# A fused two-layer graph network on one core: the stores move from GpSimd's queue to SyncE's and ScalarE's

## The chip, the cores and the metric

The kernel runs on one core of a Trainium2 chip. A core has a matrix engine (TensorE, PE in the profile), three engines for elementwise work (VectorE, DVE; ScalarE, ACT; GpSimd, POOL) and SyncE (SP), which only issues transfers. Transfers between device memory and on-chip memory run on 16 DMA engines that all issuing engines share. In this program three engines issue them: SyncE, ScalarE and GpSimd. The metric is the device time of one execution in microseconds (us), lower is better. All data are float32.

## The reference, cut to what matters

The inputs are x (3327 x 512), a dense symmetric matrix adj (3327 x 3327), and the weights of two layers.

```python
h = relu(layernorm(x))
q, k, v = h @ Wq.T + bq, h @ Wk.T + bk, h @ Wv.T + bv
a = q @ k.T / sqrt(512) + adj + adj
x = x + softmax(a, axis=-1) @ v

h = relu(layernorm(x))
A2 = adj + eye
dscale = diagonal(A2) ** -0.5
temp = A2 @ h @ W.T
x = x + relu((dscale[:, None] * A2 * dscale[None, :]) @ temp)
```

Three large products have a 3327 x 3327 left operand: the softmax's numerators with h, A2 with the second h, and A2 with temp. Before the first, the scores are a product of 3327 x 512 with 512 x 3327.

## The kernel before, in words

The rows are padded to 3328, which is 26 tiles of 128 rows. Products are made in the way of Strassen and Winograd: a product of 2 x 2 blocks is done as seven block products with sums and differences of blocks before and after. VectorE makes these sums. Everything that is too large for on-chip memory goes through scratch tensors in device memory: `rowd[g]` (the right operands' rows for product g), `qd` (queries), `pd` (exponentials of the scores and their block sums), `sumd` (block sums of adj), `totd` (row totals), `t2d` (one difference of right operands, used by a later block product), `x1d` (x after the first layer). A store writes such a tensor, a load brings a part of it back later.

The stages follow each other:

* The head (L286 to L379). It makes M from the query and key weights, normalises x tile by tile (`h_transposed`; the row tile goes to `rowd[0]`, L324), transposes it, and computes the queries (`project_q`, stored at L362).
* The scores (L384 to L568). 52 steps, each a `Pair`: load two blocks of adj (`adjacency`, L418), seven products (L454), add the adjacency, exponentiate, make block sums, and store: `sum` (L446), the exponentials in four stores (L462, L481, L485, L490). At the end of each of four groups, row totals are stored (L514). The next group's queries are loaded at L399. A buffer that is loaded into for a later pair is one that an earlier pair has stored from.
* Three products (L577 to L1045), g = 0, 1, 2. Each has seven block products in the order p5, p1, p6, p7, p2, p3, p4, each of these two strips of output columns, and each strip seven steps, 294 steps in all. `run(k)` writes one step: it issues the loads of the left operand for step k+3 (`Step.load`, by `left`, L694 to L701), the matmuls of step k (L774 and L782), the sums for step k+2 on VectorE (`four_sums`, L173 to L175), and at the end of a strip the gathering of the results into the output's blocks (`Gather`, L811 to L840). Behind that come the items that `between[k]` holds: the right operand of a later strip is loaded five steps ahead and made three steps ahead (`Right`, rows loaded at L721; for p6 a store of `t2`, L746); 52 jobs that add a block of adj to a stored sum and store the result (`Job`, loads L860 and L861, add L865, store L868; they run from the second strip of g = 0 into g = 1); `attend` (residual and layernorm after g = 0, stores `x1d`, L888), `attended` (L894), `temp` (product with W, L874, store L903) and `finish` (transposes L927, relu L929, residual L930, store `out`, L931 through `store` at L92).
* After the last step, six half tiles of the output are finished, stored in turn by GpSimd and SyncE (L1044 and L1045). Row 25 holds 127 rows, and `store` writes it in two pieces, 112 and 15 rows.

The order of each engine's instructions in the scores and in the products is the order in which this program writes them: `in_order` ties each instruction to the one before it on the same engine. So an engine that has to wait with one instruction holds up all that is written behind it on that engine. Rings of buffers set when a load may start: the left operand has five buffers, its sums three; a load waits until the buffer's last reader is done.

All stores but three of the last output tiles are issued by GpSimd. SyncE issues nearly all loads. ScalarE issues 65 loads (weights and x in the head, x and `x1d` in the products). GpSimd also makes some memsets, masks and 53 small powers for the layernorms.

`general_kernel` (L1049 on) lies in a branch for other data, which isn't taken.

Of the kernel before, what the change touches and what calls it, by code (L numbers as in the profile page):

```python
# [47 lines left out]
def graph_layers_kernel(  # L48
# [38 lines left out]
        m = n - n % 16  # L87
        return [(0, m), (m, n)] if m and m < n else [(0, n)]

    def store(dst, src, n, queue=nc.gpsimd):  # L90
        for a, z in pieces(n):
            queue.dma_start(dst[a:z], src[a:z])  # L92

# [222 lines left out]
    def h_transposed(k):  # L316

        a, n = PACKS[k]
        for _, i in (o for o in order if o[0] == k):
            xt = first.pop(i) if i in first else load_x(i)  # L320
            rstd, bias = norm(xt)
            ht = n_ring([P, D], "ht")
            nc.scalar.activation(ht, xt, AF.Relu, bias=bias(), scale=rstd)
            nc.gpsimd.dma_start(rowd[0][ROW[i]], ht)  # L324
            pt = tp_bank("tp").rearrange("p (c e) -> p c e", c=DC)
            for c in range(DC):
                nc.tensor.transpose(pt[:, c], ht[:, c * P : (c + 1) * P], ident)
            w = slice((i % HALF - a) * P, (i % HALF - a + 1) * P)
            if i < HALF:
                nc.scalar.copy(hp[k][:, 0:2, :, w], pt.rearrange("p (a c) e -> p a c e", a=2))  # L330
            else:
                nc.scalar.copy(hp[k][:, 2, :, w], pt[:, 2:4])
                nc.vector.tensor_add(hp[k][:, 3, :, w], hp[k][:, 2, :, w], pt[:, 0:2])
                nc.vector.tensor_add(hp[k][:, 5, :, w], hp[k][:, 0, :, w], pt[:, 0:2])
        nc.vector.tensor_add(hp[k][:, 4], hp[k][:, 3], hp[k][:, 0])
        nc.vector.tensor_add(hp[k][:, 6], hp[k][:, 1], hp[k][:, 4])

    def project_q(k):
        a, n = PACKS[k]
        w = n * P  # L340

        qs = [half(8 + j, [P, 2, BW], "qs") for j in range(4)]

        def chain(o):
            def product(ps, name, start):
                for c in range(2):
                    nc.tensor.matmul(ps[:, :w], M[B[name]][:, c, o * P : (o + 1) * P], hp[k][:, A[name], c],  # L347
                                     start=start and c == 0, stop=c == 1, skip_group_check=True)

            def first(j, ps, sign):  # L350
                d = 2 * (j % 2) + o
                nc.scalar.activation(qs[j][:, o, :w], ps[:, :w], AF.Identity, bias=u[:, d : d + 1], scale=float(sign))

            def more(j, ps):
                nc.vector.tensor_add(qs[j][:, o, :w], qs[j][:, o, :w], ps[:, :w])

            def last():
                if o == 1:
                    for j in range(4):
                        y, z = divmod(j, 2)  # L360
                        i = ROW[y * HALF + a] * P
                        nc.gpsimd.dma_start(qd[:, 2 * z : 2 * z + 2, i : i + w], qs[j][:, :, :w])  # L362

            Chain(product, first, more, last)

        for o in range(2):
            chain(o)
# [53 lines left out]
    class Pair:  # L421
# [11 lines left out]
        def sum_of_adjacency(self, m):  # L433
# [9 lines left out]
                if d:  # L443
                    nc.vector.tensor_add(o[:, d[0]], o[:, d[0]], d[1])
            if m == 1:
                nc.gpsimd.dma_start(self.to(sumd)[:, 0:2], self.o)  # L446

        def multiply(self, qt):
            wd, g = self.wd, self.g
# [7 lines left out]
            def first(n, ps, sign):  # L457
                nc.vector.scalar_tensor_tensor(a[n], a[n], 2.0, ps[:, :wd], op0=ALU.mult,  # L458
                                               op1=ALU.add if sign > 0 else ALU.subtract)
                if n == 2:  # L460
                    nc.scalar.activation(g[1], g[1], AF.Exp, **({"bias": pad} if self.t == HALF - 1 else {}))  # L461
                    nc.gpsimd.dma_start(self.to(pd)[:, 0:2], g[1])  # L462
                beside[{0: 0, 3: 1, 1: 3, 2: 4}[n]]()

            def more(n, ps):
# [12 lines left out]
        def s1(self):  # L478
            s1 = self.g[0][:, 1]
            nc.vector.tensor_add(s1, s1, self.g[1][:, 1])  # L480
            nc.gpsimd.dma_start(self.to(pd)[:, 2:4], self.g[0])  # L481

        def s2(self):
            nc.vector.tensor_add(self.e[:, 1], self.g[0][:, 0], self.g[0][:, 1])
            nc.gpsimd.dma_start(self.to(pd)[:, 4:6], self.e)  # L485

        def s4(self):
            self.last = fours[:, self.t % 2, : self.wd]
            nc.vector.tensor_add(self.last, self.e[:, 1], self.g[1][:, 0])
            nc.gpsimd.dma_start(self.to(pd)[:, 6], self.last)  # L490

        def gather(self, m):

# [8 lines left out]
        def total(self, m, own=None):  # L502
# [8 lines left out]
            else:  # L511
                nc.vector.tensor_sub(row, ps[:1, : self.wd], acc[:1, 0])
            c0 = (STRIPS[self.s] + (1 - m) * HT[self.s]) * P + self.c
            nc.gpsimd.dma_start(totd[:, c0 : c0 + self.wd], row)  # L514


    pairs = {}
# [52 lines left out]
    def totals():  # L570
        for m in range(2):
            pairs[len(steps_of_scores) - 1].total(m, bank(ROLE["p8"], "tot"))
        nc.sync.dma_start(tot, totd[0].rearrange("(i p) -> p i", p=P))

    steps_of_scores = steps
# [87 lines left out]
    b_ring = ring(*((half, k) for k in (0, 1, 2, 3, 8, 9, 10)))  # L663
    r_ring = ring(*((half, k) for k in (4, 5, 6, 7)))
    cts = {}

    def set_up():

# [38 lines left out]
    class Right:  # L707
# [31 lines left out]
        def make(self):  # L739
# [3 lines left out]
            if r == "p6":  # L743
                nc.vector.tensor_add(own, own, self.two[:, :, 0:E])
                nc.vector.tensor_sub(own, own, self.two[:, :, E:D])
                nc.gpsimd.dma_start(self.t2[:, 0 : 2 * self.n], self.b[:, 0 : 2 * self.n])  # L746
            if r in ("p7", "p4"):
                nc.vector.tensor_sub(own, own, self.one)
            if self.n == 2:
# [100 lines left out]
    class Job:  # L850
# [13 lines left out]
        def make(self):  # L864
            nc.vector.tensor_add(self.a, self.a, self.b)  # L865
            if self.d:
                nc.vector.tensor_add(self.a[:, self.d[0]], self.a[:, self.d[0]], self.d[1])
            nc.gpsimd.dma_start(sumd[self.s][self.j][:, 2 + self.k], self.a)  # L868

    def times_weights(i, w):  # L870
        s, y, k = where(i)
# [11 lines left out]
    def attend(i):  # L883
# [1 line left out]
        xt, ps = xts[i], times_weights(i, wv_w1[0])  # L885
        nc.vector.scalar_tensor_tensor(xt, ps, rs[:, i : i + 1], xt, op0=ALU.mult, op1=ALU.add)  # L886
        nc.vector.tensor_add(xt, xt, bvs[0])
        nc.gpsimd.dma_start(x1d[i], xt)  # L888
        normed[i] = norm(xt)

    def attended(i):
        h1 = h_ring([P, D], "h1")
        nc.scalar.activation(h1, xts[i], AF.Relu, bias=normed[i][1](), scale=normed[i][0])
        nc.gpsimd.dma_start(rowd[1][i], h1)  # L894

    normed = {}

    def temp(i):
# [1 line left out]
        ps = times_weights(i, wv_w1[1])  # L900
        ts = ts_ring([P, D], "ts")
        nc.scalar.mul(ts, ps, sd[:, i : i + 1])
        nc.gpsimd.dma_start(rowd[2][i], ts)  # L903

    xrs = {}

# [9 lines left out]
            xrs[i + k] = xr[:, k]  # L916
            nc.scalar.dma_start(xr[:, k], x1d[i + k][:, 0:E])

    def finish(i, z=(0, 1), spot=None, queue=nc.gpsimd):

        s, y, k = where(i)
        n = min(P, N - i * P)
# [5 lines left out]
        o = (out_ring if spot is None else out_last)([P, D], "r")  # L928
        nc.scalar.activation(o[:, c0:c1], pt[:, c0:c1], AF.Relu, scale=sd[:, i : i + 1])  # L929
        nc.vector.tensor_add(o[:, c0:c1], o[:, c0:c1], xr[:, c0:c1])  # L930
        store(out[i * P : i * P + n, c0:c1], o[:n, c0:c1], n, queue)  # L931

    every = (*range(PAIRS), None)
    rights = {(g, r, t): Right(g, r, t) for g in range(3) for r in ORDER for t in every}
# [62 lines left out]
        rows(2, number_of(2, 4, 0, t), i, (1,))  # L997
    for n, i in enumerate(range(20, NT, 2)):
        at(number_of(2, 6, 1, 2) + n, last_load, i)
    for k, what in ((1, totals), (2, prepare), (6, prepared), (8, judge), (9, judged)):  # L1000
        at(k, what)
    at(number_of(1, 1, 0, 4), other_weights)

# [8 lines left out]
    def run(k):  # L1012
        step = steps[k]
        if k + 3 < len(steps):
            steps[k + 3].load()
        if step.t == 0:
            banks_of.update(seven())
        if not cts:
# [22 lines left out]
    with in_order(*(e.engine for e in (nc.vector, nc.tensor, nc.gpsimd, nc.scalar, nc.sync))):  # L1041
        for k in range(len(steps)):
            run(k)
        for n, i in enumerate(range(20, NT)):  # L1044
            finish(i, (0,), (0, 2, 4, 6, 7, 1)[n], (nc.gpsimd, nc.sync)[n % 2])  # L1045
    return flags[0]

@with_exitstack
def general_kernel(  # L1049
# [49 lines left out]

    def store(dst, src, n):  # L1100
        for a, z in pieces(n):
            nc.gpsimd.dma_start(dst[a:z], src[a:z])

    const = ctx.enter_context(tc.tile_pool(name="const", bufs=1))
    held = ctx.enter_context(tc.tile_pool(name="held", bufs=1))
# [316 lines left out]
```

## Time and profile before

| | |
|---|---|
| Time, median of 5 runs | 2210.8 us (2210.39 to 2214.28) |
| The profiled execution: its time | 2210.64 us |
| Its span, first to last instruction | 2208.7 us |
| TensorE clock granted | 0.996 of full speed |
| Transfers issued by SyncE, GpSimd, ScalarE | 1185, 491, 65 |
| Bytes moved | 583.68 MB, mean 264 GB/s |
| Scores, 150 to 580 us: TensorE busy, DMA share, rate | 429.43 us of 430, 0.85, 301 GB/s |
| Product g = 0, 680 to 1000 us | 318.07 us of 320, 0.88, 313 GB/s |
| 1240 to 1500 us, in product g = 1 | 258.07 us of 260, 0.88, 310 GB/s |
| 1500 to 1900 us | 400.00 us of 400, 0.60, 194 GB/s |
| Behind TensorE's last matmul, 2195 to 2208.7 us | VectorE 1.67 us, ScalarE 1.21 us busy |

The profile is of one execution. Its page gives each engine's busy time and share, the DMA queues (q1 is SyncE's, q10 ScalarE's, q0 GpSimd's, called software_dynamic), and the chain of work that ended last, followed back from the last instruction. The view of waits lists, for an engine, how long it waited for which instruction of which other engine; "SPq L697 <- PE p L782" is SyncE, standing at line 697, waiting for a matmul of line 782. A group's line gives the first and last start. The letter q behind an engine's name (SPq, POOLq) marks its sequencer, which handles waits and transfers. Issuing a transfer takes the issuing engine some time of its own; its landing comes later.

### The profile page before, as it was taken

What the parts mean: (1) busy time and instruction counts of PE and PEld (TensorE: products, weight loads), DVE (VectorE), ACT (ScalarE), POOL (GpSimd) and SP (SyncE); (2) the same over time, 40 slices, a digit from 0 to 9 for tenths busy, and PEclk for the clock granted to TensorE, in tenths of its full rate; (3) what the DMA queues carried; (4) which work ended last, traced back from release to release, by engine and by line L of the source; (5) the groups of instructions that cost most, each with busy time, mean ns of one, the idle gap of its engine ahead of it and who ended that gap; (6) DMA issues with size and microseconds to landing.
All of it is one profiled execution on the core that took longest, in us unless ns stands there. A gap on an engine that the chain in (4) does not pass through costs nothing.

```text
span 2208.7 us, 20973 instructions
## 1 busy us (share of the span) xinstructions
PE 2174.9 (98%) x6268; PEld 1166.9 (53%) x6268; DVE 1628.0 (74%) x3103; ACT 231.3 (10%) x335; POOL 357.5 (16%) x551
## 2 busy tenths in 40 slices
PE   9999999999999999999999999999999999999997
PEld 6555555455555555555454555555545555555554
DVE  6369888888877788877777778886645358777776
ACT  5321121112110000000001000000000000000011
POOL 5233333333331000001222100000000000000011
PEclk9999999999999999999999999999999999999999
DMA  8568888888969898888787899876645458766684
GB/s 286 188 209 300 298 296 281 304 284 309 353 211 327 302 370 305 280 291 315 254 307 264 307 347 354 282 275 199 219 141 181 135 189 295 248 192 191 207 305 169
DMA packets 246682, 583.68 MB, mean 264 GB/s; under 512 B 34768, under 2 KB 106270, under 8 KB 246558
## 3 DMA queue, kind: packets, MB, share of 16 engines
q1 hardware_dynamic: 192270, 399.28, 54.4%
q0 software_dynamic: 44928, 167.49, 19.9%
q10 hardware_dynamic: 9360, 15.47, 2.1%
q8 instruction: 52, 0.85, 0.2%
q14 instruction: 72, 0.59, 0.1%
HBM read 414.28 MB, written 167.85 MB: 264 GB/s over the span
## 4 chain that ended last, share of the span: by engine, by line
PE 89%; DVE 4%; DMA 3%; issue 3%; POOL 1%; ACT 0%; SPq 0%; ACTq 0%; POOLq 0%; DVEq 0%
PE p L782 53%; PE Y L454 12%; PE p L874 7%; PE Z L454 6%; PE p L774 5%; PE X L454 3%; DMA g<-in_adjT_dram 1%; PE Y L347 1%; PE mm L306 1%; DMA b<-row 1%; DVE part L173 1%; PE pt L927 0%; PE Z L347 0%; DVE part L174 0%; DMA qd<-qs 0%
## 5 line engine op out<-in xcount | busy, mean ns | idle before, releaser
L782 PE MATMUL p<-part,b 128*128 128x448 f32 (+1 forms) x3528 | 1252.3, 513 | 6.0 <-DVE part L174 4.9
L782 PEld LDWEIGHTS p<-part,b 128*128 128x128 f32 x3528 | 667.7, 190 | 569.8 <-issue 306.9
L173 DVE TENSOR_TENSOR part<-part 128x896 f32<-128x896 f32 (+1 forms) x252 | 257.2, 1021 | 99.0 <-PE p L782 46.6
L454 PE MATMUL Y<-qt,hp 128*128 128x448 f32 (+1 forms) x832 | 309.0, 514 | 3.8 <-DVE g L458 2.8
L454 PEld LDWEIGHTS Y<-qt,hp 128*128 128x128 f32 x832 | 157.2, 190 | 139.5 <-issue 72.3
L454 PE MATMUL Z<-qt,hp 128*128 128x384 f32 (+1 forms) x416 | 162.5, 513 | 0.0
L175 DVE TENSOR_TENSOR part<-part,part 128x448 f32<-128x448 f32 (+1 forms) x219 | 129.5, 591 | 16.9 <-DVE part L174 0.5
L174 DVE TENSOR_TENSOR part<-part,part 128x448 f32<-128x448 f32 (+1 forms) x219 | 129.4, 591 | 7.4
L774 PE MATMUL p<-part,b 128*128 128x448 f32 (+1 forms) x336 | 124.2, 513 | 0.0
L874 PE MATMUL p<-w,ct 128*128 128x512 f32 x272 | 123.5, 593 | 0.5 <-DVE part L886 0.5
L454 PEld LDWEIGHTS Z<-qt,hp 128*128 128x128 f32 x416 | 78.8, 190 | 67.4 <-issue 37.4
L458 DVE SCALAR_TENSOR_TENSOR g<-g,Y 128x384 f32<-128x384 f32 (+1 forms) x156 | 91.4, 586 | 28.9 <-PE Y L454 25.7
L868 POOL DMA_DIRECT2D sum<-job x52 | 28.4, 547 | 500.8 <-DVE job L865 283.4
L811 DVE TENSOR_TENSOR part<-p,part 128x384 f32<-128x384 f32 (+1 forms) x33 | 19.4, 587 | 103.9 <-PE p L782 103.1
L774 PEld LDWEIGHTS p<-part,b 128*128 128x128 f32 x336 | 63.6, 190 | 53.8 <-issue 32.4
L810 ACT COPY part<-p 128x384 f32<-128x384 f32 (+1 forms) x33 | 16.6, 503 | 682.9 <-PE p L782 682.0
L874 PEld LDWEIGHTS p<-w,ct 128*128 128x128 f32 x272 | 51.5, 190 | 59.7 <-issue 51.9
L454 PE MATMUL X<-qt,hp 128*128 128x384 f32 (+1 forms) x208 | 81.1, 512 | 0.0
L461 ACT ACTIVATE g<-g 128x768 f32<-128x768 f32 (+1 forms) x48 | 43.0, 896 | 353.5 <-DVE g L458 294.5
L446 POOL DMA_DIRECT2D sum<-o x52 | 36.9, 709 | 221.5 <-DVE o L440 152.9
L874 PE MATMUL p<-w,part 128*128 128x512 f32 x144 | 65.7, 592 | 0.0
L92 POOL DMA_DIRECT2D out_dram<-r x30 | 16.2, 542 | 302.2 <-DVE r L930 267.3
(165 smaller groups left out, 1881.7 us busy)
## 6 DMA issues: line engine op xcount, KB each, us to landing
part<-sum SPq DMA_DIRECT2D x104, 448.0 KB, 5.0
part<-p SPq DMA_DIRECT2D x91, 448.0 KB, 6.4
part<-sum SPq DMA_DIRECT2D x104, 384.0 KB, 3.5
part<-p SPq DMA_DIRECT2D x91, 384.0 KB, 4.3
part<-in_adjT_dram SPq DMA_DIRECT2D x78, 448.0 KB, 4.6
b<-row SPq DMA_DIRECT2D x234, 128.0 KB, 5.0
part<-in_adjT_dram SPq DMA_DIRECT2D x78, 384.0 KB, 3.7
g<-in_adjT_dram SPq DMA_DIRECT2D x52, 448.0 KB, 4.6
```

Source lines behind the costliest of these rows:

```text
L173: nc.vector.tensor_add(o[:, 0:2], g[:, 0:4:3], g[:, 1:2].to_broadcast([P, 2, g.shape[-1]]))
L174: nc.vector.tensor_add(o[:, 2], o[:, 1], g[:, 0])
L175: nc.vector.tensor_add(o[:, 3], o[:, 2], g[:, 2])
L306: nc.tensor.matmul(ps[r], w_q[c // 2][:, c % 2, r * P : (r + 1) * P], w_k[c // 2][:, c % 2], start=c == 0, stop=c == DC - 1)
L446: nc.gpsimd.dma_start(self.to(sumd)[:, 0:2], self.o)
L454: nc.tensor.matmul(ps[:, :wd], h_of(self.t, name, k), qt[B[name]][:, k], start=start and k == 0, stop=k == 1, skip_group_check=True)
L458: nc.vector.scalar_tensor_tensor(a[n], a[n], 2.0, ps[:, :wd], op0=ALU.mult, op1=ALU.add if sign > 0 else ALU.subtract)
L461: nc.scalar.activation(g[1], g[1], AF.Exp, **({"bias": pad} if self.t == HALF - 1 else {}))
L774: yield nc.tensor.matmul(ps[("p2", "p3", "p4", "p8")[k]][:, :w], b[:, z], a[:, 0, y], start=k == 3, stop=True)
L782: yield nc.tensor.matmul(ps[r][:, :w], b[:, i], m, start=self.t == 0, stop=self.t == PAIRS - 1 and r in ("p1", "p5", "p6", "p7"))
L868: nc.gpsimd.dma_start(sumd[self.s][self.j][:, 2 + self.k], self.a)
L874: nc.tensor.matmul(ps, cts[s][y][d][:, k * P : (k + 1) * P], w[d], start=d == 0, stop=d == DC - 1)
```

## The change

GpSimd issues no transfer any more.

* In the head and in the scores, each store is issued by SyncE at the same place in the program.
* In the products, the stores of `t2`, of the jobs, of `x1d` and of `out` are put on a list (`posted`). In the next `run`, SyncE issues them (`deliver`), behind the loads that this step issues first. The stores of h1 and ts are issued by ScalarE, which makes these rows, in place.
* The load of the row totals comes one step later than the computation that stores them.
* The six last half tiles are posted and delivered together at the end: the fourth and the fifth by ScalarE, the others by SyncE.

After it SyncE issues about 1620 transfers, ScalarE 119 and GpSimd none.

```diff
 
-    def store(dst, src, n, queue=nc.gpsimd):
+    def store(dst, src, n, queue=nc.sync):
         for a, z in pieces(n):
...
             nc.scalar.activation(ht, xt, AF.Relu, bias=bias(), scale=rstd)
-            nc.gpsimd.dma_start(rowd[0][ROW[i]], ht)
+            nc.sync.dma_start(rowd[0][ROW[i]], ht)
             pt = tp_bank("tp").rearrange("p (c e) -> p c e", c=DC)
...
                         i = ROW[y * HALF + a] * P
-                        nc.gpsimd.dma_start(qd[:, 2 * z : 2 * z + 2, i : i + w], qs[j][:, :, :w])
+                        nc.sync.dma_start(qd[:, 2 * z : 2 * z + 2, i : i + w], qs[j][:, :, :w])
 
...
             if m == 1:
-                nc.gpsimd.dma_start(self.to(sumd)[:, 0:2], self.o)
+                nc.sync.dma_start(self.to(sumd)[:, 0:2], self.o)
 
...
                     nc.scalar.activation(g[1], g[1], AF.Exp, **({"bias": pad} if self.t == HALF - 1 else {}))
-                    nc.gpsimd.dma_start(self.to(pd)[:, 0:2], g[1])
+                    nc.sync.dma_start(self.to(pd)[:, 0:2], g[1])
                 beside[{0: 0, 3: 1, 1: 3, 2: 4}[n]]()
...
             nc.vector.tensor_add(s1, s1, self.g[1][:, 1])
-            nc.gpsimd.dma_start(self.to(pd)[:, 2:4], self.g[0])
+            nc.sync.dma_start(self.to(pd)[:, 2:4], self.g[0])
 
         def s2(self):
             nc.vector.tensor_add(self.e[:, 1], self.g[0][:, 0], self.g[0][:, 1])
-            nc.gpsimd.dma_start(self.to(pd)[:, 4:6], self.e)
+            nc.sync.dma_start(self.to(pd)[:, 4:6], self.e)
 
         def s4(self):
             self.last = fours[:, self.t % 2, : self.wd]
             nc.vector.tensor_add(self.last, self.e[:, 1], self.g[1][:, 0])
-            nc.gpsimd.dma_start(self.to(pd)[:, 6], self.last)
+            nc.sync.dma_start(self.to(pd)[:, 6], self.last)
 
...
             c0 = (STRIPS[self.s] + (1 - m) * HT[self.s]) * P + self.c
-            nc.gpsimd.dma_start(totd[:, c0 : c0 + self.wd], row)
+            nc.sync.dma_start(totd[:, c0 : c0 + self.wd], row)
 
...
             pairs[len(steps_of_scores) - 1].total(m, bank(ROLE["p8"], "tot"))
+
+    def load_totals():
         nc.sync.dma_start(tot, totd[0].rearrange("(i p) -> p i", p=P))
...
     cts = {}
+    posted = []
+
+    def post(dst, src):
+        posted.append(lambda: nc.sync.dma_start(dst, src))
+
+    def deliver():
+        while posted:
+            posted.pop(0)()
 
...
                 nc.vector.tensor_sub(own, own, self.two[:, :, E:D])
-                nc.gpsimd.dma_start(self.t2[:, 0 : 2 * self.n], self.b[:, 0 : 2 * self.n])
+                post(self.t2[:, 0 : 2 * self.n], self.b[:, 0 : 2 * self.n])
             if r in ("p7", "p4"):
...
                 nc.vector.tensor_add(self.a[:, self.d[0]], self.a[:, self.d[0]], self.d[1])
-            nc.gpsimd.dma_start(sumd[self.s][self.j][:, 2 + self.k], self.a)
+            post(sumd[self.s][self.j][:, 2 + self.k], self.a)
 
...
         nc.vector.tensor_add(xt, xt, bvs[0])
-        nc.gpsimd.dma_start(x1d[i], xt)
+        post(x1d[i], xt)
         normed[i] = norm(xt)
 
     def attended(i):
         h1 = h_ring([P, D], "h1")
         nc.scalar.activation(h1, xts[i], AF.Relu, bias=normed[i][1](), scale=normed[i][0])
-        nc.gpsimd.dma_start(rowd[1][i], h1)
+        nc.scalar.dma_start(rowd[1][i], h1)
 
...
         nc.scalar.mul(ts, ps, sd[:, i : i + 1])
-        nc.gpsimd.dma_start(rowd[2][i], ts)
+        nc.scalar.dma_start(rowd[2][i], ts)
 
...
 
-    def finish(i, z=(0, 1), spot=None, queue=nc.gpsimd):
+    def finish(i, z=(0, 1), spot=None, queue=nc.sync):
 
...
         nc.vector.tensor_add(o[:, c0:c1], o[:, c0:c1], xr[:, c0:c1])
-        store(out[i * P : i * P + n, c0:c1], o[:n, c0:c1], n, queue)
+        posted.append(lambda: store(out[i * P : i * P + n, c0:c1], o[:n, c0:c1], n, queue))
 
...
         at(number_of(2, 6, 1, 2) + n, last_load, i)
-    for k, what in ((1, totals), (2, prepare), (6, prepared), (8, judge), (9, judged)):
+    for k, what in ((1, totals), (2, load_totals), (2, prepare), (6, prepared), (8, judge), (9, judged)):
         at(k, what)
...
             steps[k + 3].load()
+        deliver()
         if step.t == 0:
...
             run(k)
+        deliver()
         for n, i in enumerate(range(20, NT)):
-            finish(i, (0,), (0, 2, 4, 6, 7, 1)[n], (nc.gpsimd, nc.sync)[n % 2])
+            finish(i, (0,), (0, 2, 4, 6, 7, 1)[n], nc.scalar if n in (3, 4) else nc.sync)
+        deliver()
     return flags[0]
```

The one other store, in `general_kernel`, moves from GpSimd to SyncE in the same way.

More of the change, by code (lines that the diff above doesn't have):

```diff
@@ L1101, in store @@
         for a, z in pieces(n):
-            nc.gpsimd.dma_start(dst[a:z], src[a:z])
+            nc.sync.dma_start(dst[a:z], src[a:z])
     const = ctx.enter_context(tc.tile_pool(name="const", bufs=1))
```

## The prediction

> **What bounds the kernel now.** I read the page first: which engine is full, who carries the transfers, and the chain that ended last.
>
> ```profile
> PE 2174.9 (98%) x6268; PEld 1166.9 (53%) x6268; DVE 1628.0 (74%) x3103; ACT 231.3 (10%) x335; POOL 357.5 (16%) x551
> q1 hardware_dynamic: 192270, 399.28, 54.4%
> q0 software_dynamic: 44928, 167.49, 19.9%
> PE 89%; DVE 4%; DMA 3%; issue 3%; POOL 1%; ACT 0%; SPq 0%; ACTq 0%; POOLq 0%; DVEq 0%
> ```
>
> TensorE is busy for 98% of the span, so a change that touches no matmul can act in two ways only: through the few microseconds in which TensorE waits, and through what lies before its first and behind its last matmul. POOL has 1% of the chain, and q0, GpSimd's queue, carries all the stores. The second view is what TensorE's idle time waited for:
>
> ```profile
> PE p L782 <- DVE part L174: 4.9, 4, 1.9
> PE pt L927 <- DVE part L840: 3.1, 2, 2.5
> PE Y L454 <- DVE g L458: 2.8, 4, 1.1
> PE Y L347 <- ACT qs L352: 1.8, 1, 1.8
> ```
>
> The first number is the total in us, then the times and the longest one. All releasers are VectorE or ScalarE; no wait here is charged to a store. The third view is the end, by the groups of the program's closing lines and the timeline:
>
> ```profile
> 2194.42 2.25 DVE L930 TENSOR_TENSOR r<-r,xr 128x256 f32<-128x256 f32 x6 [1.04 <-ACT r L929]
> 2195.24 2.33 SPq L92 DMA_DIRECT2D out_dram<-r  x4
> 2196.60 0.55 POOL L92 DMA_DIRECT2D out_dram<-r  x1 [0.19 <-issue]
> ...
> L1418 SPq EVENT_SEMAPHORE  x8: 17/17/17, 2200.2 to 2201.4; - x8
> L1418 POOLq INC_SWDGE_SEM  x1: 1516/1516/1516, 2200.9 to 2200.9; - x1
> ...
> L1414 SPq EVENT_SEMAPHORE  x14: 17/28/28, 2202.4 to 2208.7; - x14
> L1414 POOLq DRAIN  x3: 40/107/5459, 2202.5 to 2208.5; - x3
> ```
>
> The last result is ready at 2196.67 and SP's last store (15 rows) is issued at 2197.09. SP has seen its stores land by 2201.4, starts its final waits at 2202.4 when GpSimd has closed its software transfers (a 1.516 us instruction), and is done at 2203.17. Then everything waits for one GpSimd DRAIN of 5.459 us, 2202.45 to 2207.91, and 0.83 us of barrier end the span at 2208.74. So 13.7 us lie behind the last matmul (2194.96), and 5.5 of them are this DRAIN.
>
> The fourth view is what SP, the engine that gets the stores, waits for today:
>
> ```profile
> SPq L418 <- DMA p<-g: 441.0, 48, 48.3
> SPq L697 <- PE p L782: 316.2, 131, 9.2
> SPq L860 <- DMA sum<-job: 31.5, 9, 7.8
> SPq L573 <- DMA totd<-acc: 25.7, 1, 25.7
> ```
>
> SP spends most of its time waiting for a buffer to come free; it has time to issue more, but it issues in order.
>
> **The change part by part.** The sum is made against the profiled execution: 2210.64 us, span 2208.7 and 1.94 around it. It stands 0.16 below the median of 2210.8.
>
> *The end.* Removed: GpSimd's three last stores, the 1.516 us closing instruction, the software completions SP waits for (4 of its 12 final ones). Added: one more store on SP, two on ScalarE. SP's list becomes rows 0, 1, 2 and the two pieces of the last tile; its stores cost 0.34 to 0.47 us and the results come every 0.37 us, so the 15-row piece is again issued near 2197.1 and seen by 2201.4. Then eight waits, which now stand 0.06 us apart (2202.37, 2202.43, ...): 2201.4 + 0.07 + 8 x 0.06 + 0.06 = 2202.0, and 0.83 of barrier: 2202.85, which is 5.9 less. This needs the DRAIN to be short. If it keeps its 5.46 us but starts when GpSimd has nothing left (2197.1), it ends at 2202.5 and the end is 2203.4: 5.3 less. If it keeps them and comes behind SP's last wait, 2202.0 + 5.46 + 0.83 = 2208.3: 0.4 less. The other DRAIN rows of GpSimd, behind no transfers, take 40 and 107 ns; they are nearest, and I take -5.8, bounds -5.9 and -0.4.
>
> *The head.* 26 row stores (0.58 us each on GpSimd) and 16 query stores (0.72 us) go to SP, whose nearest issue, the query load, costs 0.42. The TensorE wait of 1.8 us at 96 us is a chain: four query stores, the query load (SP issues it at 91.7), ScalarE's use of it at 96.4, which holds up L352. Four issues at 0.42 for 0.72 bring the load forward by up to 1.2 us. Against it: the loads of x now stand in SP's queue behind the row stores, and in the new order some are 2 to 8 us later between 28 and 40 us, where VectorE would lag by up to 4 us; TensorE waited 0.5 to 0.7 there twice. Bounds -1.2 and +3; I take -0.4, as the row of the wait is a measured one and the lag has a lead before it.
>
> *The scores.* Five stores a step, 260 in all, and 8 of totals: 5 x 0.4 = 2.0 us of SP in a step of 10 us, in which SP waits 441/52 = 8.5 us for L418. They come in the order in which the results come, so no load waits for a store that is not yet computed; a store may wait behind a load for a landing of 3 to 4 us (GpSimd's score stores land in 3.4 us by the median), and the buffers it frees are wanted a step, 10 us, later. Cover: that step. Bounds: -4.4 (all the idle time TensorE has between 579 and 651 us) and +3 (as many waits of 0.6 to 1.1 again); I take 0. The totals' load goes one step later; it held SP for 25.7 us (L573), but its stores, now on SP too, hold it as long: 0.
>
> *The products.* 52 job stores, 21 of t2 and, from attend and finish, 26 and 27 more are issued by SP after the next step's loads. A store that isn't computed yet now blocks the loads behind it. I put the new order of SP's queue against the old times at which each store was issued: at some 30 places loads come 3 to 13 us later, the worst near 788 us, where loads of the right operand go from 788.4 to 795.6 behind a t2 and a job store. They are needed at 798.3, at a time when transfers are slow:
>
> ```profile
> 770.00:800.00 30.00, 30.00 (x81) 15.20 (x80) 26.63 (x51) 0.53 (x1) 3.78 (x7) 1.00 1.04 406
> 800.00:850.00 50.00, 50.00 (x147) 27.74 (x146) 43.77 (x77) 0.48 (x1) 2.16 (x4) 1.00 0.98 354
> 1300.00:1340.00 40.00, 40.00 (x114) 21.37 (x113) 35.96 (x69) 0.48 (x1) 5.26 (x10) 1.00 1.04 403
> ```
>
> (Columns: window, length, busy time of PE, its weight loads, DVE, ACT and POOL, clock, DMA share, GB/s.) The DMA engines are full here, and VectorE has 11% of its time left at 770 to 800. What late loads cost TensorE is not in the trace. From above: at five places (805, 881, 912, 1423, 1455 us, changes of strip) VectorE finishes only 0.1 to 3 us before TensorE needs it; 3 us lost at each is +15. From below 0, and the nearest row says so: SP is blocked in just this manner already, by L860, which waits 7.79 us at 972.4 and 4.54 at 1255.7 for a job store to land; TensorE has no idle time in the 50 us after either. At 1449.8 it waits 7.01, and TensorE loses 0.86 at 1455. I take +1 for blocking. Stores also get dearer: q0 moves 167.49 MB in 19.9% (8.4 MB a point), q1 399.28 in 54.4% (7.3), so 15% more for 19.9 points, 3 of 100; over the 150 us or so that are full that is 4.5 us of transfer, of which TensorE's lead takes most: +0.5, bounds 0 and 4.5, within the +15. The 26 stores of h1 and 26 of ts on ScalarE, which is 10% busy, delay nothing on a path: 0.
>
> The Trainium skill, "DMA: Bandwidth & Descriptors", section "Queues, rings and completion order", speaks against the change: an engine takes turns between queue rows packet by packet, while within one row descriptors are taken in ring order, so loads that today run beside a store would stand behind it. The share of 1.04 at 770 us with both queues active doesn't contradict it, and no run here shows one row alone. By that rule a 448 KB store at 400 GB/s is an estimated 1.1 us ahead of the loads; at the five thin places that is 5 us more, and the sum would be about 2211.
>
> Sum: 2210.64 - 5.8 - 0.4 + 0 + 1.5 = 2205.9, with the 0.16 to the median 2206.1; I say 2206.0.
>
> **The rivals.**
> *Blocked loads decide (slower side).* In the p6 and p7 strips of the first two products SP stands in front of an uncomputed store, the right operands and sums come late to a VectorE that has 11 to 20% to spare, and TensorE waits at the changes of strip. For: the thin leads and the full windows. Against: the L860 row. Seven to ten waits of 1.5 to 2 us are 10 to 20: 2206.0 - 1.5 + (10 to 20), or 2214 to 2224. It decides from 6.2 us on, where it eats the whole gain of the end and the head.
> *The DRAIN stays.* It is GpSimd's own closing work, paid whatever it did, and comes last: 2210.64 - 0.4 - 0.4 + 1.5 = 2211.3. For: nothing in the trace ties it to transfers. Against: the 40 and 107 ns rows.
> *All goes well.* End -5.9, head -1.2, and the score waits shrink by half of 4.4, nothing lost in the products: 2201.3; with half of these extras 2203. For: SP issues faster than GpSimd. Against: no wait is charged to a store.
>
> **How the numbers follow.** A measurement here tells no change from one within 0.2%, 4.4 us: faster is below 2206.4, slower above 2215.2. My forecast (the products cost 0 to 3, 2204.5 to 2207.5) 0.43, of which 0.28 fall below 2206.4; all goes well 0.15, faster; the DRAIN stays 0.09, same; blocked loads 0.33, of which 0.06 below 2215.2. Faster 0.43, same 0.15 + 0.09 + 0.06 = 0.30, slower 0.27. The range 2202 to 2222 leaves out some 0.05 at either end. The forecast's own range is 2204.5 to 2207.5.
>
> **What would show it.** The end: span minus TensorE's last end falls from 13.7 to about 8, no GpSimd DRAIN over 1 us. The head: the wait L347 on L352 below 1.8. The scores: waits of L454 near 2.8 in sum. The products: TensorE's waits on VectorE at L782 stay below 4.9 + 1.9 + 1.5 or so, while SP shows new waits for DVE job L865 and DVE b L745. The forecast is wrong if TensorE's last end moves by over 5 us, or if the DRAIN stands at 5.4 behind SP's last wait.

## The result, and the profile after

The changed kernel is slower by a quarter of a percent: 2217.92 us median (2212.72 to 2224.26, 30 runs) against 2212.28 us (2208.96 to 2216.58, 51 runs) for the kernel before. The ratio is 1.0025, with a 95% interval of 1.002 to 1.003. The profiled execution took 2219.43 us, its span is 2217.0.

On the page of the changed kernel, GpSimd's queue q0 is gone and SyncE's q1 has its bytes:

```profile
PE 2182.7 (98%) x6268; PEld 1171.8 (53%) x6268; DVE 1626.7 (73%) x3103; ACT 231.3 (10%) x335; POOL 47.2 (2%) x60
q1 hardware_dynamic: 282604, 552.87, 72.3%
q10 hardware_dynamic: 17136, 29.37, 3.8%
PE 88%; DVE 5%; DMA 4%; issue 1%; SPq 1%; POOL 0%; ACT 0%; DVEq 0%; POOLq 0%
```

TensorE is busy for 7.8 us more with the same 6268 matmuls. That was not expected, and the last section comes back to it. The DMA engines' share is the same as before to half a point (72.3 + 3.8 against 54.4 + 19.9 + 2.1).

Matmul for matmul, the two traces differ as follows (the changed kernel's start less that of before). I read this table first, since it says in which stage the time went.

| up to | matmul (counted from 0) | before, us | after, us | difference | gained or lost in the stage |
|---|---|---|---|---|---|
| end of the head | 500th | 149.11 | 146.87 | -2.24 | -2.24 |
| first steps of the products | 2000th | 685.19 | 681.73 | -3.46 | -1.22 |
| g = 0, to 859 us | 2500th | 858.73 | 859.07 | +0.34 | +3.80 |
| g = 0, to 964 us | 2800th | 964.34 | 971.16 | +6.82 | +6.48 |
| from there through g = 1 | 4200th | 1475.68 | 1489.13 | +13.44 | +6.62 |
| last matmul's end | 6268th | 2194.96 | 2209.17 | +14.21 | +0.77 |
| end of the span | | 2208.74 | 2217.0 | +8.3 | -5.9 |

So the end won 5.9 us, head and scores won 3.5, and the products lost 17.7. The closing lines show the first of these. Before, the longest DRAIN of GpSimd's closing was 5459 ns; now it is 82, and SyncE's last waits (2215.7 on) are followed at once by the barrier:

```profile
L1431 SPq EVENT_SEMAPHORE  x8: 17/17/17, 2215.1 to 2215.6; - x8
...
L1427 SPq EVENT_SEMAPHORE  x10: 17/28/28, 2215.7 to 2216.9; - x10
L1427 POOLq DRAIN  x3: 34/45/82, 1248.2 to 2216.7; - x3
```

TensorE's waits (line numbers are 10 higher here from the products on: L792 is L782 of before):

```profile
PE p L792 <- DVE part L174: 9.5, 5, 2.7
PE p L792 <- DVE part L837: 5.1, 5, 2.0
...
PE Y L454 <- DVE g L466: 2.1, 1, 2.1
PE p L792 <- DVE part L821: 1.9, 2, 1.0
```

The first line was 4.9 before, the second 0.9 (L827 there), the fourth wasn't there. L837 and L821 gather a strip's results, L174 is behind the sums of the next one: these are changes of strip. The wait of L347 on L352 (1.8 us in the head) is gone. The view of SyncE's waits has what is new. L671 is the line that issues a posted store:

```profile
SPq L707 <- PE p L792: 204.3, 100, 9.1
SPq L671 <- DVE job L875: 146.5, 26, 12.1
...
SPq L418 <- DMA p<-g: 104.9, 47, 6.5
...
SPq L671 <- DVE job L877: 55.9, 11, 8.7
```

By these two rows SyncE stands 202 us before job stores whose sum isn't made yet, up to 12.1 us at a time. (The view puts some waits at the same stores down to other instructions of VectorE; with these it is 250 us.) One of these places, in the timelines of SyncE, VectorE and TensorE of the changed kernel:

```profile
885.10 0.56 SPq L704 DMA_DIRECT2D part<-p  x1
890.79 0.32 SPq L671 DMA_DIRECT2D sum<-job  x1
891.21 0.90 SPq L731 DMA_DIRECT2D b<-row  x2
892.16 0.50 SPq L870 DMA_DIRECT2D job<-sum  x1
892.70 0.43 SPq L871 DMA_DIRECT2D job<-in_adjT_dram  x1
893.23 0.85 SPq L704 DMA_DIRECT2D part<-p  x2
...
906.87 0.32 SPq L671 DMA_DIRECT2D sum<-job  x1
```

```profile
887.68 0.96 DVE L173 TENSOR_TENSOR part<-part 128x768 f32<-128x768 f32 x1 [3.14 <-DMA part<-p]
...
889.81 0.95 DVE L875 TENSOR_TENSOR job<-job 128x768 f32<-128x768 f32 x1
...
893.54 0.28 DVE L183 TENSOR_TENSOR b<-b 128x128 f32<-128x128 f32 x1
900.37 1.09 DVE L173 TENSOR_TENSOR part<-part 128x896 f32<-128x896 f32 x1 [6.55 <-DMA part<-p]
...
905.89 0.95 DVE L875 TENSOR_TENSOR job<-job 128x768 f32<-128x768 f32 x1
906.75 0.55 DVE L837 TENSOR_TENSOR part<-part,p 128x384 f32<-128x384 f32 x1
```

```profile
907.36 9.29 PE L792 MATMUL p<-part,b 128*128 128x448 f32 x24 [1.25 <-DVE part L837]
919.38 2.90 PE L792 MATMUL p<-part,b 128*128 128x448 f32 x7 [2.73 <-DVE part L174]
```

SyncE issues its last load at 885.10 and stands before the job store. VectorE, which has itself waited 3.14 us for an earlier load, makes the job's sum at 889.81 to 890.76, SyncE stores it at 890.79, and only then issues the loads behind it, the left operand's two at 893.23. VectorE has nothing to do from 893.8 and waits 6.55 us for them. It is late with the next job's sum (905.89), which SyncE can store only at 906.87, and with the strip's gathering (906.75), and TensorE stops for 1.25 and then for 2.73 us. In the kernel before GpSimd issued the corresponding job store, and SyncE's loads of the left operand went out every 4.5 us:

```profile
886.97 0.54 POOL L868 DMA_DIRECT2D sum<-job  x1 [6.63 <-DVE job L865]
```

```profile
883.90 1.61 SPq L694 DMA_DIRECT2D part<-p  x2
...
888.41 1.61 SPq L694 DMA_DIRECT2D part<-p  x2
...
892.93 1.61 SPq L694 DMA_DIRECT2D part<-p  x2
```

### The profile page after: what moved, and what is told of

It is laid out like the page before. It is cut to its first block, busy times and chain, and to the rows that moved or that the text cites. A ratio compares the mean times of both kernels' runs of the same rounds, so it can differ in the third digit from the quotient of the medians.

```text
span 2217.0 us, 20535 instructions
## 1 busy us (share of the span) xinstructions
PE 2182.7 (98%) x6268; PEld 1171.8 (53%) x6268; DVE 1626.7 (73%) x3103; ACT 231.3 (10%) x335; POOL 47.2 (2%) x60
## 3 DMA queue, kind: packets, MB, share of 16 engines
q1 hardware_dynamic: 282604, 552.87, 72.3%
## 4 chain that ended last, share of the span: by engine, by line
PE 88%; DVE 5%; DMA 4%; issue 1%; SPq 1%; POOL 0%; ACT 0%; DVEq 0%; POOLq 0%
PE p L792 50%; PE Y L454 13%; PE p L884 7%; PE Z L454 7%; PE p L784 4%; PE X L454 3%; PE Y L347 2%; DMA part<-p 1%; DMA b<-row 1%; PE Z L347 1%; DVE part L173 1%; DMA xt<-in_x_dram 1%; DMA rows<-row 1%; DMA part<-sum 0%; PE pt L937 0%
## 5 line engine op out<-in xcount | busy, mean ns | idle before, releaser
L792 PE MATMUL p<-part,b 128*128 128x448 f32 (+1 forms) x3528 | 1259.1, 515 | 16.9 <-DVE part L174 9.5
L792 PEld LDWEIGHTS p<-part,b 128*128 128x128 f32 x3528 | 670.6, 191 | 585.6 <-issue 309.8
L174 DVE TENSOR_TENSOR part<-part,part 128x448 f32<-128x448 f32 (+1 forms) x219 | 129.5, 591 | 7.4
L458 DVE SCALAR_TENSOR_TENSOR g<-g,Y 128x384 f32<-128x384 f32 (+1 forms) x156 | 91.6, 587 | 31.7 <-PE Y L454 28.4
L821 DVE TENSOR_TENSOR part<-p,part 128x384 f32<-128x384 f32 (+1 forms) x33 | 19.3, 585 | 80.2 <-PE p L792 41.3
L454 PEld LDWEIGHTS X<-qt,hp 128*128 128x128 f32 x208 | 39.6, 190 | 33.0 <-issue 19.3
L875 DVE TENSOR_TENSOR job<-job 128x896 f32<-128x896 f32 (+1 forms) x52 | 53.0, 1018 | 2.0 <-DMA job<-in_adjT_dram 2.0
L200 POOL TENSOR_TENSOR rstd<-ve,mhalf 128x1 f32<-128x1 f32 x52 | 41.2, 794 | 582.4 <-DVE ve L198 551.6
```

The costliest lines, as they stand in the source:

```text
L174: nc.vector.tensor_add(o[:, 2], o[:, 1], g[:, 0])
L200: nc.gpsimd.tensor_tensor(rstd, ve, mhalf, op=ALU.pow)
L454: nc.tensor.matmul(ps[:, :wd], h_of(self.t, name, k), qt[B[name]][:, k], start=start and k == 0, stop=k == 1, skip_group_check=True)
L792: yield nc.tensor.matmul(ps[r][:, :w], b[:, i], m, start=self.t == 0, stop=self.t == PAIRS - 1 and r in ("p1", "p5", "p6", "p7"))
```

## The experiments

Two theories for the 17.7 us of the products. Theory 1: SyncE issues in order and stands before stores that are not computed yet, so the loads behind come late. Theory 2: loads and stores now share one queue, and stores are dearer there. A third question was what the DRAIN at the end belongs to.

**The job and t2 stores two steps later.**

```diff
+    def post_late(dst, src):
+        late.append((now[0] + 2, lambda: nc.sync.dma_start(dst, src)))
...
+        while late and late[0][0] <= now[0]:
+            late.pop(0)[1]()
...
-                post(self.t2[:, 0 : 2 * self.n], self.b[:, 0 : 2 * self.n])
+                post_late(self.t2[:, 0 : 2 * self.n], self.b[:, 0 : 2 * self.n])
...
-            post(sumd[self.s][self.j][:, 2 + self.k], self.a)
+            post_late(sumd[self.s][self.j][:, 2 + self.k], self.a)
```

> The changed kernel, but SyncE issues the job and t2 stores one step later still, two steps behind the step that makes them. Same bytes, same queue, same ring; only the wait for an uncomputed store goes (in the changed kernel SyncE stands 146.5 + 55.9 us before job stores, L671 <- DVE job). Theory 1 (SyncE stands in front of stores that are not computed yet, and the loads behind them come late): TensorE's last end falls from 2209.2 us in the profile to 2191.5 to 2195, the time to about 2200 to 2204. Theory 2 (one queue instead of two, dearer stores): TensorE's last end stays within 3 us of 2209.2, the time near 2218.

Measured: 2201.37 us, ratio to the kernel before 0.9954 (0.9938 to 0.997). TensorE's last end is 2188.93 us, 2.6 earlier than the expected range, because head and scores won more in this run than in the changed kernel's trace. Its lead over the kernel before is 6.93 us at the 2000th matmul and 6.98 at the 5400th: up to there the products lose nothing, and behind it 0.9 us. TensorE's waits at the matmuls of the products are back at their value of before:

```profile
PE p L801 <- DVE part L174: 4.9, 4, 1.9
PE pt L946 <- DVE part L859: 3.1, 2, 2.5
```

The same bytes go by the same queue as in the changed kernel, so theory 2 falls: of its price nothing is to be seen. SyncE's waits for job results fell from 202 us to 78, not to nothing:

```profile
SPq L716 <- PE p L801: 225.3, 107, 9.1
...
SPq L676 <- DVE job L884: 63.2, 17, 9.3
```

**The job and t2 stores by ScalarE.**

```diff
+    def post_late(dst, src):
+        late.append((now[0] + 1, lambda: nc.scalar.dma_start(dst, src)))
...
         for what, args in between.get(k, ()):
             what(*args)
+        deliver_late()
```

> The changed kernel, but the job and t2 stores are issued by ScalarE at the end of the next step, so they stand in front of no load of SyncE and go by ScalarE's own queue. Theory 1 (late loads behind uncomputed stores): as for the two-step kernel, TensorE's last end at 2191.5 to 2195, the time 2200 to 2204. Theory 2 (the stores and loads share one queue): the same gain, since these 448 KB stores leave SyncE's queue. So if the two-step kernel stays slow and this one is fast, theory 2 holds. If both are slow, it is neither.

Measured: 2202.28 us, ratio 0.9952 (0.9938 to 0.9965), the last end at 2194.3 us: it has two more stretches at half speed (last section) than the kernel above, a wait of 1.4 us in the scores that is 0.3 there, and one more of 1.7. On another queue the same gain as on the same queue two steps later. What counts is what stands behind the store, not which queue carries it.

**SyncE made to wait, without the bytes.**

```diff
+    def post(src):
+        posted.append(lambda: nc.sync.dma_start(scrap, src))
...
                 nc.gpsimd.dma_start(self.t2[:, 0 : 2 * self.n], self.b[:, 0 : 2 * self.n])
+                post(self.b[:1, 0, 0:16])
...
             nc.gpsimd.dma_start(sumd[self.s][self.j][:, 2 + self.k], self.a)
+            post(self.a[:1, 0:16])
```

> The kernel before, with all its stores on GpSimd, and one thing more: in the products SyncE also issues, a step later and behind the loads, a store of 16 numbers that depends on each job's and each t2's result, where the changed kernel has the store itself. SyncE is made to wait as in the changed kernel, but moves 64 bytes. Theory 1: TensorE stalls in the first two products as in the changed kernel, its last end 10 to 18 us behind the 2195.0 us of before, the time 2221 to 2229. Theory 2 (queue and bytes): within 3 us of before, about 2212.

Measured: 2249.03 us in one run, the last end at 2233.19, 38 us behind before. The stores are on GpSimd as before, and SyncE's waits alone bring the stalls:

```profile
SPq L670 <- DVE job L875: 204.9, 34, 12.6
...
SPq L670 <- DMA scrap<-b: 33.7, 12, 6.9
```

```profile
PE p L792 <- DVE part L174: 17.2, 10, 3.7
```

That is theory 1, but over twice the price I expected. Part of the reason is my edit: all the small stores go to one scratch row, so some also wait for the landing of an earlier one (33.7 us). And SyncE stands longer before them: 302 us at those of the jobs, all releasers counted, where the changed kernel has 250. How much of the excess that makes, the run doesn't tell.

**The job stores at once, not a step later.**

```diff
-            post(sumd[self.s][self.j][:, 2 + self.k], self.a)
+            nc.sync.dma_start(sumd[self.s][self.j][:, 2 + self.k], self.a)
```

> The changed kernel, but the 52 job stores are issued by SyncE in the step that makes them, ahead of the next step's loads, not a step later. If the loss comes from how long SyncE stands before an uncomputed store, one step less of delay adds up to a step (some 4.5 us) to each of the 52 waits: SyncE's waits for job results grow from 202 us to 350 or more, and TensorE's last end goes from 2209 to 2225 or later. If a step more or less made no difference to the waits, the last end stays within 4 us of 2209.

Measured: 2272.35 us in one run, the last end at 2262.75. With the two-step kernel this makes a series in one number: job stores issued 0, 1 and 2 steps behind the step that makes them give about 2272, 2218 and 2201 us. The direction was as expected, but SyncE's waits for job results grew only to 297 us, where I had expected 350 or more (with the waits at these stores that the view puts down to other instructions they grew from 250 to 357):

```profile
SPq L878 <- DVE job L875: 214.6, 27, 17.0
...
SPq L878 <- DVE job L877: 82.7, 12, 9.6
```

```profile
PE p L792 <- DVE part L821: 24.4, 8, 3.9
PE p L792 <- DVE part L174: 18.1, 12, 4.4
```

Set beside each other, SyncE's waits for job results of 78, 202 and 297 us (two steps, one, none; 86, 250 and 357 with the other instructions) go with losses in the products (the last end's difference to before, less that at the 2000th matmul) of 0.9, 17.7 and 73.8 us. The first 78 us lie within what TensorE's lead covers; the last 95 cost 56.

**Only the job stores two steps later.** The two-step kernel with t2 posted for the next step again:

```diff
-                post_late(self.t2[:, 0 : 2 * self.n], self.b[:, 0 : 2 * self.n])
+                post(self.t2[:, 0 : 2 * self.n], self.b[:, 0 : 2 * self.n])
```

> The two-step kernel, but only the 52 job stores are issued two steps later; the t2 stores go a step later as in the changed kernel. If the job stores alone made the loads late (146.5 + 55.9 of SyncE's waits, against 30.7 + 7.1 for t2), TensorE's last end is within 2 us of the two-step kernel's 2188.9. If the t2 stores have a share, the stalls near 802, 836 and 1384 us are partly back and the last end is at 2192 or later.

Measured: the last end at 2189.26 us, 0.3 from the two-step kernel, 2199.94 us. The job stores alone made the loss; t2, which I had named beside them, has no share that shows. Neither have the stores of `x1d` and `out`: SyncE stands 82.1 and 68.6 us before them in the changed kernel (`L671 <- DVE part L897`, `L92 <- DVE r L940`), 94.3 and 68.6 in this one, whose products lose 0.9 us in all. The same kernel again, timed:

> The kernel with only the job stores two steps later once more, timed. From its first profile (TensorE's last end 2189.3 us, 6 to 8 us behind it and 2 around the span) the time is 2199 to 2202, a ratio to the kernel before of 0.994 to 0.997: head and scores -6.7, end -4 to -6, products 0.

Measured: 2200.13 us (2198.4 to 2202.87), ratio 0.9943 (0.9923 to 0.9964). This is the fastest version found by its median (the two-step kernel's 2201.37 lies within the spread of these runs), and differs from the changed kernel in the step at which 52 stores are issued. Its profiled execution, the slowest of the six at 2202.87 us, loses 3.4 us in the products, nearly all behind the 5400th matmul, with half clock behind the stop near 1986 us and near 2191.

**The products' part of the change alone** (head and scores store by GpSimd):

```diff
-                nc.sync.dma_start(self.to(pd)[:, 2:4], self.g[0])
+                nc.gpsimd.dma_start(self.to(pd)[:, 2:4], self.g[0])
```

and so for the other stores of head and scores.

> The change in the products and at the end alone: head and scores store by GpSimd as before. Theory 1 (SyncE blocked by uncomputed job stores, all of it in the products): TensorE's last end 13 to 19 us behind the 2195.0 of before, since the products lost 17.9 in the changed kernel and head and scores won 3.5 that are not won here. GpSimd's last store is then that of the row totals near 652 us; if the closing DRAIN is paid only for stores near the end, the end stays near 7.9 us and the time is 2218 to 2224. Theory 2 (one queue for everything, built up over the whole kernel): the loss in the products is smaller than in the changed kernel by a third or more.

Measured: the last end at 2215.11 us, 20.1 behind before (19 was the end of the expected range), 2225.51 us in one run (2224 was). The stalls are those of the changed kernel (8.8 us of L174, 6.2 of L837, 5.1 of L821), so nothing builds up from the stages ahead.

**Head and scores alone** (products and end as before, the load of the row totals a step later as in the change):

```diff
-                nc.gpsimd.dma_start(self.to(pd)[:, 2:4], self.g[0])
+                nc.sync.dma_start(self.to(pd)[:, 2:4], self.g[0])
```

and so for the other stores of head and scores.

> The change in the head and the scores alone (with the totals' load one step later): in the products and at the end GpSimd stores as before. If the gains of 2.2 us by 150 us and of another 3 to 5 by 700 us belong to these stores, TensorE reaches its 2100th matmul 5 to 7 us earlier than before, keeps that lead to its last end (2188 to 2190), the end stays at 13.7 us, and the time is 2203 to 2206. If they came from elsewhere (SyncE's queue in the products), the lead is under 2 us and the time near 2211.

Measured: 2206.38 us, ratio 0.9967 (0.9956 to 0.9979). The lead is 6.68 us at the 2000th matmul and 6.72 at the 5400th. So the stores of these two stages by SyncE are a gain of their own. The end was 15.0 us, with a DRAIN of 6.19 us, longer than expected.

**The last six stores alone.**

```diff
+        what = lambda: store(out[i * P : i * P + n, c0:c1], o[:n, c0:c1], n, queue)
+        what() if spot is None else posted.append(what)
...
-            finish(i, (0,), (0, 2, 4, 6, 7, 1)[n], (nc.gpsimd, nc.sync)[n % 2])
+            finish(i, (0,), (0, 2, 4, 6, 7, 1)[n], nc.scalar if n in (3, 4) else nc.sync)
+        while posted:
+            posted.pop(0)()
```

> The kernel before with one part of the change: the last six half tiles are stored by SyncE and ScalarE, all else by GpSimd as before. GpSimd's last store is then issued near 2191.8 us instead of 2196.6. Theory A (the DRAIN of 5.46 us and the closing instruction of 1.5 us follow GpSimd's last landing and run beside SyncE's closing if that is later): landing near 2196.5, closed at 2198, drained at 2203.5, so the end is 9 to 10 us instead of 13.8 and the time 4 us below before. Theory B (GpSimd closes only when SyncE has): the end stays above 13 us. Theory C (the DRAIN is paid only when a store was issued in the last 3 to 4 us): the end is near 8 us, the time 6 below before.

Measured: 2208.58 us, ratio 0.9971 (0.9959 to 0.9983). The end is 8.93 us, and theory A describes it: GpSimd closes its transfers and drains while SyncE still waits for its own stores.

```profile
L1423 POOLq INC_SWDGE_SEM  x1: 1452/1452/1452, 2197.3 to 2197.3; - x1
```

```profile
L1419 POOLq DRAIN  x3: 40/170/5214, 2198.8 to 2206.7; - x3
L1419 SPq DRAIN  x3: 7/7/7, 2205.7 to 2206.3; - x3
```

The DRAIN still takes 5.2 us, but it begins at 2198.8 and SyncE isn't done before 2205.7. So most of the gain at the end was to be had by six stores.

**One early store by GpSimd in the changed kernel.**

```diff
-            nc.sync.dma_start(rowd[0][ROW[i]], ht)
+            (nc.gpsimd if i == 0 else nc.sync).dma_start(rowd[0][ROW[i]], ht)
```

> The changed kernel, but the first row store of the head is issued by GpSimd. If the closing DRAIN of 5.459 us belongs to any use of GpSimd's queue, however early, it is back: the end behind the last matmul is 12 to 14 us instead of 7.85, the time about 2222 to 2224. If it belongs to the stores near the end, the end stays at 7.85 us and the time near 2218.

Measured: 2216.63 us in one run, the end 8.56 us, the longest DRAIN of GpSimd's closing 140 ns. So a single early store doesn't bring the DRAIN back. But neither is it "stores near the end" that count: in the kernel with the products' part alone, whose last GpSimd store is issued at 651.4 us, GpSimd reaches its closing at 1252.4 us and drains there for 4.89 us, beside all the other work:

```profile
L1427 POOLq DRAIN  x3: 44/107/4892, 1252.4 to 2223.4; - x3
```

One store 0.14 us; 181 stores (head and scores alone moved) 6.2, 310 stores 4.9, 488 and 491 stores 5.2 and 5.5: the DRAIN comes with having used the queue for more than a store, and costs only where GpSimd comes to it last. What sets its length stays open; it isn't the number of stores alone.

## Why the prediction was wrong, point by point

**The end: right.** -5.8 was forecast, 13.78 went to 7.84, which is -5.9. The reason given (no transfers, short DRAIN) holds, and the experiments narrow it. The agreement to a tenth is luck: in the seven other kernels with these last stores the end is 7.7 to 10.0 us.

**The head: right direction, too small.** -0.4 was forecast with a bound of -1.2, -2.24 measured. The wait at 96 us went as a whole (1.80), not by the 1.2 of the stores' faster issue, and with it 1.0 of the waits at L327; 0.6 was lost elsewhere in the head. The late loads of x cost no more than that. The wait is gone in all eight kernels whose head stores by SyncE (their heads are 2.2 to 3.9 us shorter). In the three other kernels with the head as before it is 0.3 to 1.5 us and the head 1.2 us shorter to 0.1 longer, so some of the 2.24 may be chance.

**The scores: forecast 0, measured -1.2 in this trace,** and -3.5 to -4.8 in the seven other kernels whose scores store by SyncE. Three kernels whose scores store by GpSimd as before lie between -1.6 and +1.6, so the -1.2 alone would show nothing; the seven do. The four waits on L458 between 579 and 635 us (2.8 in sum) are gone in all eight. The fifth, of 0.96 us on L466 at 638, is one of 2.08 near there in the profiled execution of the changed kernel, with half clock behind it, which took most of the gain back; it lies between 0.2 and 1.5 us in the others, so it varies from execution to execution.

**The products: the failed step.** "I take +1 for blocking" (of +1.5), with the row of L860 as the reason. Measured: +17.7, of which ten new or longer waits of TensorE make 12.6 (by the distance of the matmuls' starts) and three stretches at half clock 4.6. The places were foreseen in part: six of the ten waits, 6.9 of the 12.6 us, are at four of the five thin places named (805, 881, 912, 1455); those at 837, 903 and 1377 to 1380 weren't named. Two things were wrong with the choice of the lower end.

The first is the row. At L860 SyncE waits for a job store to land, which happens whatever SyncE does. A posted store waits for VectorE's sum, and VectorE, in its own order, makes that sum behind others that wait for SyncE's loads. The wait feeds itself: late loads, late sum, later loads. In the 885 to 907 us shown above one round of it is to be seen, from the sum at 889.81 to the next at 905.89; how much of the 17.7 us the loop adds to the first delays, no run separates. A row of the same length with another releaser was no measure of it.

The second is the walk along SyncE's queue. It put the new order against the old times of the stores, at which VectorE was on time. It found the places, and as bounds 3 to 13 us were fair (12.1 is the longest wait). But with VectorE's times held fixed it couldn't show that loop, and I let it argue for the small end.

The upper bound of 15 held for the waits (12.6). The half clock was in none of the terms, and with it the loss passed the bound.

The other part of the +1.5, dearer stores and one queue, shows in no run: the two-step kernel has both and loses at most 0.9 us in the products, and the DMA engines' share did not rise (76.4% before, 76.1% after). The Trainium skill, "DMA: Bandwidth & Descriptors", section "Queues, rings and completion order", says that descriptors of one row are taken in order; the estimate of 5 us made from it doesn't show in any run here. What had its price was the order in which the issuing engine, SyncE, works.

So the case that came true is the rival "blocked loads decide", by its place and mechanism: it gave 2214 to 2224 and 0.33, and 2217.92 lies in its middle and in the range. The forecast's own range, 2204.5 to 2207.5, is missed by 10 us. With the one line of the products put right, the sum of the measured gains, 6 to 7 in head and scores and 4 to 6 at the end, is what the fastest version has: 2200.13.

## What to carry to other kernels

Before a store goes to the queue that also issues the loads, ask who computes it and whether that engine waits for this queue's loads; if so, a small slip can feed itself, and the store has to be issued late enough that its data is nearly always there (here two steps instead of one: 2218 became 2201 us). A wait of the same length in the old trace is a measure only if it has the same kind of releaser. And a closing cost of an engine is taken off the path nearly as well by letting the engine finish early as by not using it (8.9 against 7.8 us).

## What the runs showed of the hardware that was not expected

Most of TensorE's 7.8 us of additional busy time are matmuls at half speed behind a stop (1.7 us behind the stop at 632 us, 4.6 in the products). At 881.88 us the changed kernel's matmuls resume after 2.45 us; for some of the next twelve the distance is 0.64 us instead of 0.32, and the twelve take 5.67 us, where the kernel before took 3.97 behind a stop of 1.93. The windows show the granted clock (columns: window, length, busy time of PE, its weight loads, DVE, ACT, POOL, clock, DMA share, GB/s), first the changed kernel:

```profile
882.00:888.00 6.00, 6.00 (x14) 3.43 (x15) 2.72 (x5) 0.00 (x0) 0.00 (x0) 0.72 0.99 354
```

and the kernel before:

```profile
882.00:888.00 6.00, 6.00 (x20) 3.52 (x19) 5.69 (x9) 0.00 (x0) 0.54 (x1) 1.00 0.69 225
```

14 matmuls instead of 20 in 6 us, at a clock of 0.72. Over all twelve traces, behind the head, I counted the stops of TensorE that are followed by at least three matmuls at twice their distance: none of 63 stops of 0.8 to 1.65 us, 3 of 21 from 1.65 to 2.0, 17 of 22 from 2.0 to 2.6, 11 of 16 above. A stretch costs 1.2 to 3.2 us. The stop of 2.52 to 2.53 us near 2000 us, which all kernels have, was followed by it in all but the kernel before, whose time it would have raised too. So a stop of about 2 us can cost nearly twice its length, and short ones don't.

Why equal stops end differently, the granted clock in the traces shows. Behind the head it is half speed 33 times: for 3.41 us, five times for 6.83, once up to the end. Within a trace the starts of these stretches are whole multiples of 3.41 us apart. With the time divided into such pieces of 3.41 us, all 30 pieces in which TensorE stood for more than 2.01 us are followed by half speed, 4 of 17 with 1.65 to 2.01 us, and none of 123 with 0.6 to 1.65. So it counts how much of a stop falls into one piece. The stop of 2.53 us near 2000 us falls into two in the kernel before (where the half speed in its head places the pieces), with 1.64 and 1.45 us without a matmul, which is what PE's busy time lacks:

```profile
1988.40:1991.82 3.42, 1.79 (x5) 0.52 (x3) 3.34 (x4) 0.00 (x0) 0.00 (x0) 1.00 0.57 162
1991.82:1995.23 3.41, 1.96 (x6) 1.13 (x7) 3.31 (x8) 0.47 (x1) 0.00 (x0) 1.00 0.67 267
1995.23:1998.65 3.42, 3.42 (x10) 1.66 (x9) 3.35 (x8) 0.00 (x0) 0.54 (x1) 1.00 0.50 151
```

and in the two-step kernel it lies in one, with the half clock in the next:

```profile
1982.68:1986.09 3.41, 0.53 (x2) 0.14 (x1) 3.34 (x4) 0.00 (x0) 0.00 (x0) 1.00 0.02 9
1986.09:1989.50 3.41, 3.21 (x5) 1.62 (x6) 3.31 (x9) 0.47 (x1) 0.00 (x0) 0.50 0.13 38
```

The Trainium skill, "TensorE: Matmul & The Clock Gate", Part 1, says that the clock is halved after an idle window of about 3.4 us, and that the window runs freely. The halving, the 3.41 us and the fixed division are as these traces show them. But a window need not be idle as a whole: over 2.01 us of its 3.41 were enough each time, and the least that was enough is 1.70.

GpSimd's DRAIN of 4.9 to 6.2 us behind many transfers, 600 us after the last of them in one kernel, was the other surprise.
